# Four chained layers with six state scans on one core: where the state sums of a scan pair are emitted, how other work is rationed, and which engine takes the norms' statistics

## The chip, the cores and the metric

One core of a Trainium2 chip. Times are device microseconds of one execution. Engines: TensorE (PE) multiplies matrices into PSUM, VectorE (DVE), ScalarE (ACT) and GpSimd (POOL) work on elements, SyncE (SP) issues the DMAs. Each engine works through its own queue in order.

## The reference

Everything is float32; x is 2 x 1024 x 256. Four conditioned layers follow each other: a Mamba layer, a layer with one forward and one backward state space model, a linear attention, and a softmax attention with 16 heads of 16. The part that takes most of the time is the state scan, of 512 channels by 16 states by 1024 steps, once in layer 0 and twice in layer 1, for each of two batches (six scans):

```python
def step(h, inp):
    dt_t, B_t, C_t, u_t = inp
    dA = jnp.exp(dt_t[:, :, None] * A)
    h = h * dA + (dt_t * u_t)[:, :, None] * B_t[:, None, :]
    y = jnp.einsum('bdn,bn->bd', h, C_t)
    return (h, y)
...
y = jnp.transpose(ys, (1, 0, 2)) + u * D_param
```

A layer norm stands ahead of every layer, a second one inside layer 1, and one ahead of the output of each attention:

```python
mu = jnp.mean(x, axis=-1, keepdims=True)
var = jnp.mean((x - mu) ** 2, axis=-1, keepdims=True)
return (x - mu) * jax.lax.rsqrt(var + EPS) * g + b
```

## The kernel before

**Tiles of a scan.** A tile holds 32 channels by 4 states on 128 partitions and 1024 steps. A scan has 16 groups of channels times 4 groups of states, 64 tiles; `chain` walks them in pairs: pair p has tiles 2p and 2p+1, two neighbouring channel groups at the same state group k. Eight pairs make one d (128 channels), 32 pairs a scan, and the six scans make 192 pairs. One tile costs:
- `inputs`: e = (dt u) B on GpSimd (L961), into one of eight hb buffers;
- `decay`: dA = exp(dt A) on ScalarE, into one of two PSUM buffers of two banks;
- `tile`: the scan on VectorE (L968 backward, L972 forward), and then the product h C, back into the hb buffer. It runs on VectorE (L975) or, for the first tile of a pair where `far` is set, on GpSimd (L974);
- `fold`: TensorE sums the four states of each channel by a constant matrix, and over the four k in PSUM (L999, two matmuls a tile); at k = 0 `begin` starts the sum with D u (L985, and y of the forward scan in a backward one, L989), reading the buffers fu and fy, of which there is one each. After its sums, an hb buffer is free. `finish` takes the sum out of PSUM three pairs later (L1007, or a copy on ScalarE).

**The order in a pair.** `chain` emits the following by hand, and each engine keeps this order: the next input and the decay of tile 2p+1; a first slot of other work; the sums of pair p-1; the scan and product of tile 2p; the decay of 2p+2, an input and, if far, the product of 2p on GpSimd; a second slot of other work; the scan of tile 2p+1. The variable `lead` keeps VectorE and GpSimd level: it adds 2200 for a pair and what other work spent on VectorE, takes off what other work spent on GpSimd, and at 2300 or more the next pair's product is far (minus 3500). After a far pair the sums are split: those of tile 2p-1 at the usual place, those of 2p-2 behind the second slot. Loads of the next channels (`load_spread`, `load_rest`) stand between these steps on SP's queue.

**Other work.** Norms, projections, convolutions and inputs of the layers to come, and layers 2 and 3 of batch 0, are generators in one queue (`Behind`). Each `yield` ends a step; `slot(columns)` adds columns to a credit and runs steps while the credit is positive and neither ScalarE's nor GpSimd's room is used up. `RATES` has the columns per slot for each of the six scans. A step that yields `ALONE` ends its slot. `until` runs steps at once when something needed is not there yet.

**Norms.** Outside the scans, `stats` takes mean and variance by two instructions per 256-wide row on VectorE. Among the scans, `moments` does it on ScalarE: an Identity with an accumulator for the negated mean and a Square with an accumulator for the variance times 256. `root` (ScalarE) and `refine` (GpSimd among the scans) make the reciprocal root; `scaled` applies it on ScalarE.

After the sixth scan (the tail), layers 2 and 3 of batch 1 and both softmax attentions run; the change leaves their instructions as they are.

Of the kernel before, what the change touches and what calls it, by code (L numbers as in the profile page):

```python
# [18 lines left out]
P = 128  # L19
# [8 lines left out]
SLOT = {"ACT": 2500, "POOL": 1500}  # L28
LEAD = 2300

ALONE = -1

RATES = (2600, 2600, 1250, 1300, 1500, 1500)

LAG = 12

# [20 lines left out]
def kernel(ctx: ExitStack, tc: tile.TileContext, a: dict, out: bass.AP):  # L57
# [339 lines left out]
            nc.vector.bn_aggr(mv[:, j, :], st)  # L397
            spent["DVE"] += 550

    def moments(src, mv):  # L400

        for j in range(0, 4, 2):
            for k in (j, j + 1):
                act_f(
                    small_t((P, 2, D), "t2", 1)[:, 0, :], src[:, k, :], AF.Identity,
                    scale=-1.0 / D, accum_out=mv[:, k, 0:1],
                )
            for k in (j, j + 1):
                act_f(
                    small_t((P, 2, D), "t2", 1)[:, 0, :], src[:, k, :], AF.Square,  # L410
                    bias=mv[:, k, 0:1], accum_out=mv[:, k, 1:2],
                )
            spent["ACT"] += 4 * 250
            yield 320

    def root(mv):

        r = small_t((P, mv.shape[1]), "rstd", 2)
        act_f(r, mv[:, :, 1], AF.Ln, bias=eps, scale=1.0 / D if mode["scans"] else 1.0)
        act_f(r, r, AF.Exp, scale=-0.5)  # L420
        return r

    def refine(mv, r):

        q = small_t((P, mv.shape[1]), "newt", 2)
        e = nc.gpsimd if mode["scans"] else nc.vector
        if mode["scans"]:
            e.tensor_scalar(q, mv[:, :, 1], 1.0 / D, EPS, ALU.mult, ALU.add)
            e.tensor_tensor(q, q, r, ALU.mult)
            e.tensor_tensor(q, q, r, ALU.mult)  # L430
            e.tensor_scalar(q, q, -0.5, 1.5, ALU.mult, ALU.add)
            e.tensor_tensor(r, r, q, ALU.mult)
            e.tensor_tensor(q, mv[:, :, 0], r, ALU.mult)
            spent["POOL"] += 900
            return q
        e.scalar_tensor_tensor(q, mv[:, :, 1], EPS, r, ALU.add, ALU.mult)
        e.scalar_tensor_tensor(q, q, -0.5, r, ALU.mult, ALU.mult)
        e.scalar_tensor_tensor(r, q, 1.5, r, ALU.add, ALU.mult)
        e.scalar_tensor_tensor(q, mv[:, :, 0], -1.0, r, ALU.mult, ALU.mult)
        return q  # L440
# [14 lines left out]
    def normed(src, res):  # L455

        mv = small_t((P, 4 * len(src), 2), "mv", 4)
        for i, t in enumerate(src):
            if mode["scans"]:
                yield from moments(t, mv[:, ts(i, 4), :])  # L460
            else:
                stats(t, mv[:, ts(i, 4), :])
                yield
        r = root(mv)
        yield mode["least"] * 3 // 2
        q = refine(mv, r)
        yield
        for i, t in enumerate(src):
            res.append(scaled(t, r[:, ts(i, 4)], q[:, ts(i, 4)]))
            yield  # L470
# [42 lines left out]
    def projected(w, src, func, bias, res, keep=True, to=None, count=None):  # L513


        def take(m, ch, ps):
            if ch == 0:
                res.append(abuf())
            kw = {} if bias is None else {"bias": bias(m)}
            act_f(res[-1][:, ts(ch, 512)], ps, AF.Identity, **kw)  # L520

        def leave(m):
            if func is AF.Silu:
                silu(res[-1])
            if to is not None:
                save(2, to[ts(m, P), :], res[-1])
            if not keep:
                res.pop()
            if count is not None:
                later(2, lambda: count.append(m))  # L530

        def ended(m, ch, ps):
            take(m, ch, ps)
            held[0] -= 1
            if ch == 1:
                if func is AF.Silu:
                    yield ALONE
                leave(m)
                yield

        waiting = []
        for m in range(4):
            for ch in range(2):
                if len(waiting) == banks["bank"]:
                    yield from ended(*waiting.pop(0))
                waiting.append((m, ch, project(w, src, m, ch)))
                held[0] += 1
                yield
        for v in waiting:
            yield from ended(*v)  # L550
# [110 lines left out]
    def layer0(b, st):  # L661
# [43 lines left out]
        for m in range(4 if b else 0):  # L705

            dgs = abuf((P, 4, P))
            dg = [diag(col("conv_w", 4 * m + j), out=dgs[:, j, :]) for j in range(4)]
            xin, t = abuf(), abuf()

            def conv(ch):
                ps = bank()
                for j in range(4):
                    lag = j if ch == 0 else 0
                    mm(
                        ps[:, lag:], dg[3 - j], xin[:, 512 * ch + lag - j : 512 * ch + 512 - j],
                        start=(j == 0), stop=(j == 3),
                    )
                return ps

            def shifted(ch, ps):
                act_f(t[:, ts(ch, 512)], ps, AF.Identity, bias=col("conv_b", m))

            yield from pipe(
                (lambda: project(w_in[:1], xn, m, 0), lambda ps: act_copy(xin[:, :512], ps)),
                (lambda: project(w_in[:1], xn, m, 1), lambda ps: act_copy(xin[:, 512:], ps)),
                (lambda: conv(0), lambda ps: shifted(0, ps)),
                (lambda: conv(1), lambda ps: shifted(1, ps)),
            )
            yield ALONE  # L730
            silu(t)
            save(2, st["u"][ts(m, P), :], t)
            u.append(t)
            yield
# [6 lines left out]
    def layer1(b, st1, st2):  # L741
# [16 lines left out]
        def first():  # L758
# [5 lines left out]
            for v in skip:  # L764
                nc.vector.tensor_tensor(v, v, twice(cond["s1"][b], 4), ALU.mult)
                far_op(v, v, twice(cond["o1"][b], 4), ALU.add)
                yield ALONE
            yield ALONE
            o = []
            yield from normed(skip, o)  # L770
            for i, v in enumerate(skip):
# [53 lines left out]
    class Behind:  # L825
# [3 lines left out]
        def __init__(self):  # L829
            self.queue = []  # L830
            self.soon = []
            self.credit = 0
            self.alone = False

            self.room = {"ACT": 3400, "POOL": 2300}
            self.given = {"ACT": 0, "POOL": 0}
# [8 lines left out]
        def step(self):  # L845

            while self.queue or self.soon:
                if self.soon and self.soon[0][0] <= 0 and (held[0] == 0 or not self.queue):
                    self.queue.insert(0, self.soon.pop(0)[1])
                if not self.queue:  # L850
                    return 0
                at = work[0]
                try:
                    least = next(self.queue[0])
                    self.alone = least is ALONE
                    return max(work[0] - at, (least if least and least > 0 else mode["least"]))
                except StopIteration:
                    self.queue.pop(0)
            return 0

        def slot(self, columns):
# [3 lines left out]
            if mode["tail"]:  # L865
                for _ in range(columns):
                    self.step()
                return
            self.credit = min(self.credit + columns, 3 * T)
            for key, most in (("ACT", 3400), ("POOL", 2300)):  # L870
                self.room[key] = min(self.room[key] + SLOT[key], most)
            spent.update(ACT=0, POOL=0)
            while (self.queue or self.soon) and self.credit > 0:
# [6 lines left out]
                for key in self.room:  # L880
                    self.room[key] -= spent[key]
                    self.given[key] += spent[key]
                    spent[key] = 0
                if self.alone:
                    break

        def until(self, done):
            while not done():
# [12 lines left out]
    class Scan:  # L901
# [91 lines left out]
        def fold(self, d, cp, k, es):  # L993


            for ch in range(2):
                for j, e in es.items():
                    at = 64 * ch + DS * j
                    nc.tensor.matmul(  # L999
                        self.ys[d, cp][at : at + DS, :], fold, e[:, ts(ch, 512)],  # L1000
                        start=False, stop=(k == NK - 1),
                    )
# [13 lines left out]
    def chain(scans, rates, early, mid, after):  # L1016
# [11 lines left out]
                i, d, cp, k = pairs[n // 2]  # L1028
                made[kind][n] = getattr(scans[i], kind)(4 * d + 2 * cp + n % 2, k)

        def fold(p, js=(0, 1)):
            i, d, cp, k = pairs[p]
            if k == 0 and js[-1]:
                scans[i].begin(d, cp)
            scans[i].fold(d, cp, k, {j: made["inputs"].pop(2 * p + j) for j in js})

        def following(p):

# [18 lines left out]
        ahead(2, "inputs")  # L1057
        mode["scans"] = True
        spent.update(ACT=0, POOL=0, DVE=0)
        lead, far = 0, False  # L1060
        for p, (i, d, cp, k) in enumerate(pairs):
            s = scans[i]
            nxt = following(p)
# [13 lines left out]
            ahead(2 * p + 3, "inputs")  # L1077
            ahead(2 * p + 1, "decay")
            behind.slot(rates[i])

            split = far
            if p:
                fold(p - 1, (1,) if split else (0, 1))

            ended = pairs[p - 3][:3] if p > 2 and k == 2 else None
            if ended and not scans[ended[0]].gate:
# [24 lines left out]
            if k == 1 and nxt:  # L1111
                nxt[0].load_spread(nxt[1] + 1, 1)
            behind.slot(rates[i])
            if split:
                fold(p - 1, (0,))
            s.tile(4 * d + 2 * cp + 1, k, made["decay"].pop(2 * p + 1), made["inputs"][2 * p + 1])
            if final and i + 1 < len(scans):
                scans[i + 1].load_bc(k)
        fold(len(pairs) - 1)
        scans[-1].finish(3, 1)  # L1120
        flush()
# [626 lines left out]
```

## Time and profile before

| | us |
|---|---|
| runs | 2123.51, 2142.31, 2128.95; median 2128.95 |
| profiled execution | 2133.04, its span 2131.3 |
| first scan starts, last scan ends | 70.6, 1488.4 |

Busy time over the span of 2131.3 us:

```profile
PE 1695.2 (80%) x8112; PEld 619.4 (29%) x8112; DVE 1727.9 (81%) x1610; ACT 1207.7 (57%) x1839; POOL 1340.7 (63%) x649
```

Each engine has its busy time, the share of the span and the number of instructions. "PEld" is TensorE's loading of weights, beside its matmuls. [...]

In rows of groups: line, engine, operation, tile written <- tiles read, shapes, count | busy us, mean ns of one | idle us of the engine just before, and who ended it. In rows of waits: engine, tile and line that waited <- engine, tile and line that released it: us in total, times, longest.

### The profile page before, as it was taken

To read this page: it belongs to the slowest core of one execution; us is meant where nothing else is said; L and a number is where in the kernel's file an instruction comes from. 1 tells how busy PE (TensorE), PEld (TensorE's weight loads), DVE (VectorE), ACT (ScalarE), POOL (GpSimd) and SP (SyncE) were. 2 spreads that over 40 slices of the span, in tenths; PEclk is the share of its full clock that TensorE was granted. 3 is DMA by queue.
4 is the path that set the end of the run, shared out by engine and by line. 5 is a ranking of instruction groups with operands and counts; after the bars stand their busy time and mean duration, and the time that the engine had idled before them with its cause. 6 is when DMAs were issued, how large, how long until landed. Compare 5 with 4: busy or idle time off the path is not lost. (4 is left out here: it accounts for less than half of the span.)

```text
span 2131.3 us, 22942 instructions
## 1 busy us (share of the span) xinstructions
PE 1695.2 (80%) x8112; PEld 619.4 (29%) x8112; DVE 1727.9 (81%) x1610; ACT 1207.7 (57%) x1839; POOL 1340.7 (63%) x649
## 2 busy tenths in 40 slices
PE   6476876579888456887885676876999899999997
PEld 3132212123232111222231232310544333333333
DVE  4687798898899889999888898899767756777763
ACT  5557576657646456746456537643044555656665
POOL 0788798898899989999899778998100211000000
PEclk9687977679798556997875767886899999999998
DMA  3654348335583435556744244442300111010001
GB/s 111 233 193 143 105 174 296 115 122 194 202 287 133 168 112 186 174 190 211 286 142 152 98 167 156 138 137 80 119 1 1 38 19 18 24 55 1 1 1 38
DMA packets 106873, 267.55 MB, mean 126 GB/s; under 512 B 14619, under 2 KB 39068, under 8 KB 106757
## 3 DMA queue, kind: packets, MB, share of 16 engines
q1 hardware_dynamic: 106756, 266.07, 36.7%
q8 instruction: 64, 1.05, 0.2%
q14 instruction: 53, 0.43, 0.1%
HBM read 195.90 MB, written 67.90 MB: 124 GB/s over the span
## 5 line engine op out<-in xcount | busy, mean ns | idle before, releaser
L961 POOL TENSOR_TENSOR hb_t<-sp,bc 128x1024 f32<-128x1024 f32 x384 | 920.6, 2440 | 75.9 <-PE ys_t L999 37.5
L135 ACT ACTIVATE dA_t<-sp,negA 128x1024 f32<-128x1024 f32 x384 | 427.8, 1116 | 472.5 <-DVE hb_t L975 379.2
L972 DVE TENSOR_TENSOR_SCAN dA_t<-dA_t,hb_t 128x1024 f32<-128x1024 f32 x202 | 462.0, 2287 | 85.0 <-ACT dA_t L135 60.2
L999 PE MATMUL ys_t<-hb_t,fold 128*32 128x512 f32 x1536 | 378.9, 791 | 183.2 <-DVE hb_t L975 153.4
L1455 DVE TENSOR_REDUCE mh<-sc_t 128x1 f32<-128x512 f32 x512 | 327.5, 684 | 111.5 <-PE sc_t L1446 111.0
L135 ACT ACTIVATE hb_t<-sc_t 128x512 f32<-128x512 f32 x512 | 276.8, 595 | 189.9 <-PE sc_t L1446 189.7
L975 DVE TENSOR_TENSOR hb_t<-dA_t,bc 128x1024 f32<-128x1024 f32 x295 | 361.3, 1225 | 21.8
L1446 PE MATMUL sc_t<-act_t 32*128 32x512 f32 x2048 | 337.6, 653 | 11.2 <-DVE mh L1455 7.3
L974 POOL TENSOR_TENSOR hb_t<-hb_t,bc 128x1024 f32<-128x1024 f32 x89 | 211.6, 2378 | 42.2 <-DVE hb_t L972 30.4
L805 POOL TENSOR_TENSOR act_t<-act_t,row 128x1024 f32<-128x1024 f32 x8 | 18.8, 2349 | 339.4 <-PE sc_t L101 193.3
L968 DVE TENSOR_TENSOR_SCAN dA_t<-dA_t,hb_t 128x1024 f32<-128x1024 f32 x93 | 212.5, 2285 | 11.6 <-ACT dA_t L135 10.5
L999 PEld LDWEIGHTS ys_t<-hb_t,fold 128*32 128x32 f32 x1536 | 49.4, 122 | 451.0 <-DVE hb_t L975 288.7
L1486 PE MATMUL av_t<-hb_t,act_t 128*32 128x256 f32 x2048 | 164.6, 394 | 1.1 <-DVE act_t L1494 1.1
L135 ACT ACTIVATE act_t<-bank_t,cols 128x512 f32<-128x512 f32 (+1 forms) x206 | 130.1, 676 | 56.4 <-PE bank_t L97 54.6
L1446 PEld LDWEIGHTS sc_t<-act_t 32*128 32x128 f32 x2048 | 111.6, 186 | 120.8 <-issue 80.1
L97 PE MATMUL bank_t<-act_t,w_c_w 128*128 128x512 f32 x256 | 125.8, 639 | 22.0 <-ACT act_t L135 21.9
L972 DVE TENSOR_TENSOR_SCAN hb_t<-dA_t,hb_t 128x1024 f32<-128x1024 f32 x54 | 123.1, 2280 | 14.9 <-ACT dA_t L135 14.8
L143 POOL TENSOR_TENSOR act_t<-act_t 128x1024 f32<-128x1024 f32 x50 | 119.5, 2391 | 5.3 <-ACT act_t L135 5.1
L97 PE MATMUL bank_t<-act_t,w_dt_w 64*128 64x512 f32 x96 | 71.8, 878 | 38.5 <-ACT act_t L135 34.7
L1486 PEld LDWEIGHTS av_t<-hb_t,act_t 128*32 128x32 f32 x2048 | 42.2, 108 | 191.4 <-issue 178.7
L101 PE MATMUL bank_t<-ident,act_t 128*128 128x128 f32 x128 | 35.9, 435 | 70.5 <-ACT act_t L135 70.3
L1391 POOL MEMSET act_t<- 128x1024 f32 x8 | 7.6, 951 | 129.5 <-PE sc_t L1446 129.5
(179 smaller groups left out, 1851.4 us busy)
## 6 DMA issues: line engine op xcount, KB each, us to landing
sp<-dt SPq DMA_DIRECT2D x192, 512.0 KB, 5.3
dt<-act_t SPq DMA_DIRECT2D x48, 512.0 KB, 6.2
bc<-bc SPq DMA_DIRECT2D x48, 512.0 KB, 7.5
u<-act_t SPq DMA_DIRECT2D x24, 512.0 KB, 7.4
fu<-u SPq DMA_DIRECT2D x24, 512.0 KB
y<-y SPq DMA_DIRECT2D x96, 128.0 KB, 4.9
g<-act_t SPq DMA_DIRECT2D x16, 512.0 KB, 5.1
fg<-g SPq DMA_DIRECT2D x64, 128.0 KB, 3.9
```

Of the source, the lines that this page charges most:

```text
L97: nc.tensor.matmul(o, w, x, **kw)
L135: nc.scalar.activation(o, x, func, **kw)
L143: nc.gpsimd.tensor_tensor(o, x, y, op)
L961: nc.gpsimd.tensor_tensor(e, self.sp[c, 1], self.bc[0][k], ALU.mult)
L968: nc.vector.tensor_tensor_scan(h[:, ::-1], dA[:, ::-1], e[:, ::-1], 0.0, ALU.mult, ALU.add)
L972: nc.vector.tensor_tensor_scan(h, dA, e, 0.0, ALU.mult, ALU.add)
L974: return lambda: nc.gpsimd.tensor_tensor(e, h, self.bc[1][k], ALU.mult)
L975: nc.vector.tensor_tensor(e, h, self.bc[1][k], ALU.mult)
L999: nc.tensor.matmul(self.ys[d, cp][at : at + DS, :], fold, e[:, ts(ch, 512)], start=False, stop=(k == NK - 1),)
L1446: nc.tensor.matmul(ps, w[r, ts(at, P)], x[r, ts(wide_at, 512)], start=True, stop=True)
L1455: nc.vector.tensor_reduce(mh[n][:, t, ch, j : j + 1], ps, AX.X, ALU.max)
L1486: nc.tensor.matmul(sums.av[32 * j : 32 * j + 32, ts(part, 256)], sts[b]["v"][t // 2][:, t % 2, 4 * g + j, :], es[j // 2][:, at : at + 256] ...
```

## The change

Five parts:
- `fold` of pair p-1 moves from the middle of pair p to its end, behind the second slot and behind the second tile; the split after a far pair goes.
- `RATES` of the first two scans go from 2600 to 2048, and the credit's cap from 3 x 1024 to 2 x 1024 columns.
- `ALONE` goes: these steps become plain yields, which no longer end a slot.
- `moments` goes: among the scans too, the norms take `stats` on VectorE, all four rows of a tile of 4 x 256 in one step.
- `root` and `refine` follow the new form of the statistics; `refine` among the scans has one more GpSimd instruction.

```diff
-RATES = (2600, 2600, 1250, 1300, 1500, 1500)
+RATES = (2048, 2048, 1250, 1300, 1500, 1500)
...
-    def moments(src, mv):
...
-        act_f(r, mv[:, :, 1], AF.Ln, bias=eps, scale=1.0 / D if mode["scans"] else 1.0)
+        act_f(r, mv[:, :, 1], AF.Ln, bias=eps)
...
         if mode["scans"]:
-            e.tensor_scalar(q, mv[:, :, 1], 1.0 / D, EPS, ALU.mult, ALU.add)
+            e.tensor_scalar(q, mv[:, :, 1], EPS, None, ALU.add)
...
-            e.tensor_tensor(q, mv[:, :, 0], r, ALU.mult)
+            e.tensor_scalar(q, mv[:, :, 0], -1.0, None, ALU.mult)
+            e.tensor_tensor(q, q, r, ALU.mult)
...
         for i, t in enumerate(src):
-            if mode["scans"]:
-                yield from moments(t, mv[:, ts(i, 4), :])
-            else:
-                stats(t, mv[:, ts(i, 4), :])
-                yield
+            stats(t, mv[:, ts(i, 4), :])
+            yield
...
                 if func is AF.Silu:
-                    yield ALONE
+                    yield
...
-            yield ALONE
+            yield
             silu(t)
...
                 far_op(v, v, twice(cond["o1"][b], 4), ALU.add)
-                yield ALONE
-            yield ALONE
+                yield
...
-                    self.alone = least is ALONE
-                    return max(work[0] - at, (least if least and least > 0 else mode["least"]))
+                    return max(work[0] - at, least or mode["least"])
...
-            self.credit = min(self.credit + columns, 3 * T)
+            self.credit = min(self.credit + columns, 2 * T)
...
-                if self.alone:
-                    break
...
             behind.slot(rates[i])
-            split = far
-            if p:
-                fold(p - 1, (1,) if split else (0, 1))
...
             behind.slot(rates[i])
-            if split:
-                fold(p - 1, (0,))
             s.tile(4 * d + 2 * cp + 1, k, made["decay"].pop(2 * p + 1), made["inputs"][2 * p + 1])
             if final and i + 1 < len(scans):
                 scans[i + 1].load_bc(k)
+            if p:
+                fold(p - 1)
         fold(len(pairs) - 1)
```

## The prediction

> **What bounds the kernel now.** I read first the table of busy times by stretch, cut where the last scan ends on VectorE (1488 us), because the change touches only the scans' stage and the attention behind it keeps its instructions.
>
> ```profile
> core 0: us, PE busy (x) PEld busy (x) DVE busy (x) ACT busy (x) POOL busy (x), PEclk, DMA share, GB/s
> 70.00:1488.00 1418.00, 1043.15 (x3292) 349.28 (x3292) 1263.92 (x762) 837.57 (x1183) 1279.65 (x601) 0.77 0.49 170
> 1488.00:2131.00 643.00, 609.89 (x4712) 248.40 (x4712) 438.76 (x806) 335.14 (x605) 54.23 (x34) 0.96 0.10 26
> ```
>
> In the 1418 us of scans VectorE (DVE) is busy 89% and GpSimd (POOL) 90%: two engines share the bound, and the code keeps them level by hand ("far" products). ScalarE (ACT, 59%) and TensorE (PE, 74%) have room. From 1488 us on TensorE is 95% busy and nothing there changes, so I carry 643 us over and argue about the 1418 alone.
>
> Second, who VectorE and GpSimd wait for in that stage (line, releaser, us in total, times, longest):
>
> ```profile
> DVE dA_t L972 <- ACT dA_t L135: 60.2, 27, 5.9
> DVE dA_t L972 <- POOL hb_t L961: 24.8, 11, 13.3
> DVE hb_t L972 <- ACT dA_t L135: 14.8, 5, 5.8
> DVE act_t L812 <- PE bank_t L97: 12.1, 5, 4.7
> ```
>
> ```profile
> POOL hb_t L961 <- PE ys_t L999: 37.5, 18, 8.6
> ```
>
> With two smaller rows (10.5 and 3.0) VectorE waits 88.5 us for ScalarE's exponentials, 25.8 for GpSimd, 19 for TensorE. GpSimd waits 37.5 us because the state sums (L999) have not yet freed one of the eight hb buffers. Third, the groups by shape, for prices (busy us, mean ns):
>
> ```profile
> L961 POOL TENSOR_TENSOR hb_t<-sp,bc 128x1024 f32<-128x1024 f32 x384 | 920.6, 2440 | 75.9 <-PE ys_t L999 37.5 <-DMA bc<-bc 19.1 <-DVE y L1007 7.7
> ...
> L975 DVE TENSOR_TENSOR hb_t<-dA_t,bc 128x1024 f32<-128x1024 f32 x295 | 361.3, 1225 | 21.8
> ...
> L974 POOL TENSOR_TENSOR hb_t<-hb_t,bc 128x1024 f32<-128x1024 f32 x89 | 211.6, 2378 | 42.2 <-DVE hb_t L972 30.4 <-DVE hb_t L968 11.7
> ...
> L135 ACT ACTIVATE t<-act_t,mv 128x256 f32<-128x256 f32 x64 | 32.5, 508 | 2.1
> ...
> L135 ACT ACTIVATE t<-act_t 128x256 f32<-128x256 f32 x64 | 26.2, 409 | 1.1
> ...
> L396 DVE BATCH_NORM_STATS2 st<-act_t 128x6 f32<-128x256 f32 x48 | 19.2, 400 | 1.9 <-DMA act_t<-in_x 1.9
> ...
> L397 DVE BATCH_NORM_AGGREGATE mv<-st 128x2 f32<-128x6 f32 x48 | 8.7, 182 | 1.6
> ```
>
> **Norms' statistics.** Counting instructions in the two built programs: 64 rows' worth of statistics leave ScalarE and reach VectorE, 48 statistics become 112. VectorE gains 64 x (0.400 + 0.182) = 37.2 us. ScalarE loses 64 x (0.508 + 0.409 + 2 x 0.187 for the two accumulator reads) = 82.6 us. Of VectorE's waits for ScalarE, only two (scans 182 and 183, 1.6 and 0.9 us) lie behind such statistics; the others lie behind evictions, silu tables and the eight scalings of a norm, which stay. So ScalarE's relief is worth 2.5 us, not 82.6. The code answers the 37.2 us by its balance: `lead` counts the statistics and sends more products to GpSimd. The built programs have 89 far products before and 99 after. VectorE: 37.2 - 10 x 1.225 = **+25.0 us**. GpSimd: 10 x 2.378 + 8 small operations x 0.2 = **+25.4 us**. Both bounds rise alike.
>
> How much of the 25 shows depends on how unevenly it falls. I priced every engine's instructions between two scans by the rows above (a scan 2.285), added up groups of consecutive pairs, and took the larger of VectorE and GpSimd in each group. Example, pairs 38 to 41 (layer 1's two norms of batch 0): before 30.0 (6.5 + 5.8 + 10.7 + 7.0 on VectorE) against 29.9 on GpSimd; after 38.3 (12.5 + 7.7 + 12.3 + 5.8) against 38.0. Over the stage: all in one sum 1302 before and 1328 after (+25); groups of four pairs 1377 and 1412 (+35); single pairs 1470 and 1518 (+48). The measured 1418 lies between the last two kinds, eight hb buffers being about three pairs of lookahead, so I take groups of four: **+35**, ends +25 and +48.
>
> A rule speaks against moving more products to GpSimd. VectorE's 295 products last 1223 to 1226 ns, with GpSimd busy 90% of the stage, so I charge no contention. The Trainium skill ("GPSIMD Engine Reference", Specifications) has the two engines share SBUF interfaces, with contention when a VectorE instruction has two SBUF inputs; by it ten more GpSimd products could hold VectorE ten times, and the sum would be some 24 us higher.
>
> **State sums at the end of the next pair.** Before, the sums of pair p-1 stand on TensorE between the two slots of other work of pair p (or half of them at the end, where a product was far); after, all four, with `begin`'s two to four matmuls, stand behind both slots. Nothing is added. What it can give: TensorE's other matmuls no longer queue behind a sum that waits for VectorE (153.4 us of TensorE's waiting, 65 times). But when ScalarE waited for an eviction's bank, TensorE was mostly running that slot's own matmuls; sums running inside those waits come to about 20 us, half of the waits reach VectorE: at most -10. What it can cost: hb buffers come free later. Setting, in the trace, each sum behind the last other matmul of its second slot, the input that reuses its buffer would be late 54 times by 134 us in all, never over 11.4. These are not additive: a dense stretch loses its lead once, by about 5 us, and the median lead of an input over its scan is 8.3 us. In the stretches where GpSimd has no lead (around 300, 570, 690, 980 us) the buffers have 10 us and more to spare, so there it costs nothing. I take one loss of 5 us at three or four of the stretches, less 8 for the freed matmuls: **+8**, ends -10 and +45 (a third of 134). `begin` frees the fu and fy buffers later too, and the next loads of these, on SP's queue, stand right behind it: 24 times, half a pair (3.7 us) later each, with the spread loads queued after them. Those are needed one and a half pairs (11 us) later and land in 5.3, so this is covered; if not, it costs as the waits for sp do today (ScalarE 34.4 us in 7 waits, of which 6 us reached VectorE): +3 at the high end. The gated finish on VectorE comes three pairs behind and keeps over a pair of cover.
>
> **Rations.** 2600 becomes 2048 columns a slot for the first two scans, the credit is capped at two instead of three rows of 1024, and a slot no longer ends at `ALONE`. 2048 columns (four matmuls of 512, two rows of the trace each) take 3.70 us at best, in the timeline at 525 us, half a pair 3.51 (2.285 + 1.225). Half-pairs with over 2048 columns of other work fall from 20 to 10, and the columns above that from 27,600 to 8,700, most of it in the first two scans, where VectorE waits 62 of its 88.5 us. The 12,800 columns fewer there are 23 us of TensorE; I take half of it for VectorE's waits: **-10**, ends 0 and -41 (two thirds of 62). Against it, the 20 silus of these stages now share their slot with the eviction ahead of them, 0.68 us each, where a table load already makes VectorE wait: **+4**, ends 0 and 14.
>
> A second rule bears on the clock. The stage's granted clock is 0.77, the attention's 0.96; waits for sums average 2.4 us, the longest 6.5, and a wait for GpSimd's product reaches 6.5; I leave the clock as it is. The Trainium skill ("TensorE: Matmul & The Clock Gate", What's actually happening) has the clock halve after an idle window of some 3.4 us; one collected wait a pair would then hold it at half, TensorE's 1043 busy us would become 1043 x 0.77 / 0.5 = 1606, more than the stage lasts, and the sum some 190 us higher.
>
> **Sum.** 35 - 2.5 + 8 - 10 + 4 = +34. The profiled execution took 2133.0 us (span 2131.3, 1.7 around it), 4 above the median 2128.95 of the runs; on the median the forecast is 2163.
>
> **Rivals.**
> - Faster: TensorE's slots were the true cause of VectorE's waits. Place: 70 to 600 us, where ScalarE waits 73 us for TensorE's banks and VectorE 62 for ScalarE. If two thirds go, 25 - 41 = -16: 2113. It decides once more than 35 us of the 88.5 go. For it: 4096-column slots nearly vanish; against: silu tables and norm scalings (some 38 us of the 88.5) stay. Chance 0.10.
> - No change seen: the added VectorE work falls into its 130 us of waiting, as both engines sit idle a tenth of the time: 2129 to 2140. Against it: the two idle at different times, and a wait for ScalarE ends only after VectorE's own product. Chance 0.22.
> - Worse: the late sums starve GpSimd of buffers in the dense stretches, and a third of the 134 us reaches VectorE: 34 - 8 + 45 = +71, 2200. For it: GpSimd waits 18 times for sums already. Chance 0.13.
> - That the change does not do what it says is excluded by the built program: the counts above are its own.
>
> My forecast, both engines 25 us fuller and less even, has 0.55; its own range is 2143 to 2183. The range 2118 to 2200 takes in the ends of the terms and leaves out the far half of the fast rival and of the slow one, some 2 in 10 with the tails. About 1% (21 us, the spread of the three runs being 19) can be told from no change: below 2108 0.07, within 0.28, above 2150 0.65.
>
> **What would show it.** In the changed profile, up to the last scan: VectorE some 25 us busier, GpSimd too, ScalarE 83 less; the stage near 1452 us instead of 1418 and the attention again 643. TensorE's waits for products shrink or gather at the pair's end; GpSimd's wait for ys_t grows from 37.5 to 50 or 80. VectorE's wait for ScalarE below 50 would prove the fast rival's mechanism; GpSimd's wait for ys_t over 100, with VectorE waiting for hb_t over 60, the slow one's. I am wrong in kind if the stage is no longer while VectorE's busy time has grown.

## The result, and the profile after

The changed kernel takes 2119.66 us in the median of 16 runs (2109.82 to 2130.65), the kernel before 2140.16 in 16 (2123.51 to 2144.44). The ratio is 0.9916, with a 95% interval of 0.9899 to 0.9933: 18 us faster, where 34 us slower was forecast. Of the three runs of before that the prediction had seen, two are the fastest of the sixteen, so their median of 2128.95, on which the forecast stands, is 11 us low.

The profiled execution has a span of 2115.4 us, 15.9 under that of before. The two stretches, cut where the last scan now ends (columns as in the prediction):

```profile
70.00:1475.00 1405.00, 976.72 (x3292) 348.63 (x3292) 1281.65 (x881) 769.58 (x927) 1295.73 (x618) 0.77 0.50 171
1475.00:2115.00 640.00, 608.00 (x4712) 247.46 (x4712) 438.12 (x805) 335.40 (x605) 53.76 (x34) 0.96 0.10 26
```

The scans take 1405 us instead of 1418 (forecast: 1452), although VectorE is 18 us busier (1263.92 before) and GpSimd 16 (1279.65). ScalarE is 68 us less busy and TensorE 66, the latter with as many matmuls as before. The attention differs by 3 us, with unchanged instructions.

The waits of VectorE, GpSimd, TensorE and ScalarE that answer to those of before over the whole execution:

```profile
PE ys_t L974 <- POOL hb_t L949: 101.1, 25, 8.4
...
PE ys_t L974 <- DVE hb_t L950: 52.4, 21, 7.1
POOL hb_t L936 <- PE ys_t L974: 52.0, 20, 12.3
...
ACT act_t L133 <- PE bank_t L95: 39.6, 25, 3.9
...
DVE dA_t L947 <- ACT dA_t L133: 35.1, 18, 4.7
...
DVE dA_t L947 <- POOL hb_t L936: 27.1, 12, 13.7
...
DVE act_t L791 <- PE bank_t L95: 24.5, 7, 7.9
```

VectorE's first row was 60.2 us in 27 waits; with the smaller rows of the same kind its waits for ScalarE fall from 99 to 45 us over the scans' stage (from 88.5 to 44 for exponentials alone). It waits more for GpSimd (25.8 to 40.4 us) and for TensorE (19 to 27). GpSimd's wait for the sums grows from 37.5 to 52.0. TensorE still waits 153 us for products (183 before), now mostly for the far ones, at the end of the pair. ScalarE waits 39.6 us for TensorE's banks; before it was 60.8.

The groups:

```profile
L936 POOL TENSOR_TENSOR hb_t<-sp,bc 128x1024 f32<-128x1024 f32 x384 | 908.8, 2399 | 88.5 <-PE ys_t L974 52.0
...
L950 DVE TENSOR_TENSOR hb_t<-dA_t,bc 128x1024 f32<-128x1024 f32 x285 | 349.1, 1225 | 21.4 <-DVE dA_t L947 0.5
...
L949 POOL TENSOR_TENSOR hb_t<-hb_t,bc 128x1024 f32<-128x1024 f32 x99 | 235.7, 2381 | 19.6 <-DVE hb_t L947 17.8
```

The 285 and 99 products are the counts that the prediction worked with, at the same prices: 1225 ns on VectorE in both kernels, so the ten more far products did not slow VectorE's own.

The six scans take 242, 251, 231, 218, 240 and 225 us; before 260, 250, 231, 217, 247 and 213. The largest gain is in the first one. There, in the built program of before, four slots of the convolutions hold 4,090 columns each. ScalarE and TensorE in that stretch of the kernel before (start us, duration us, instruction and how many rows of it, [idle before <- releaser]):

```profile
219.58 0.69 ACT L135 ACTIVATE act_t<-bank_t,cols 128x512 f32<-128x512 f32 x1 [2.26 <-PE bank_t L97]
225.20 0.69 ACT L135 ACTIVATE act_t<-bank_t,cols 128x512 f32<-128x512 f32 x1 [4.93 <-PE bank_t L97]
225.79 1.11 ACT L135 ACTIVATE dA_t<-sp,negA 128x1024 f32<-128x1024 f32 x1
```

```profile
219.47 1.08 PE L985 MATMUL ys_t<-fu,dgD 64*64 64x512 f32 x4
220.48 1.05 PE L999 MATMUL ys_t<-hb_t,fold 128*32 128x512 f32 x4
221.46 3.70 PE L97 MATMUL bank_t<-act_t 128*128 128x512 f32 x8
225.09 1.91 PE L999 MATMUL ys_t<-hb_t,fold 128*32 128x512 f32 x12
```

Inside ScalarE's wait of 4.93 us (220.27 to 225.20) TensorE runs the last 1.2 us of `begin` and sums, and then the 3.7 us of the convolution whose bank ScalarE evicts. The exponential stands behind that eviction and ends at 226.9; VectorE had waited 3.24 us for it. Pairs 16 to 23, in which these convolutions fall, last 72.7 us before and 58.7 after. The largest loss is in pairs 160 to 167 (58.3 to 73.4 us): residual additions on VectorE stand there behind TensorE's banks, the last row of the waits above.

### The profile page after: what moved, and what is told of

The parts are those of the page before. It is cut to its first block, busy times and chain, and to the rows that moved or that the text cites. A ratio compares the mean times of both kernels' runs of the same rounds, so it can differ in the third digit from the quotient of the medians.

```text
span 2115.4 us, 22775 instructions
## 1 busy us (share of the span) xinstructions
PE 1626.8 (77%) x8112; PEld 617.7 (29%) x8112; DVE 1745.5 (83%) x1728; ACT 1140.4 (54%) x1583; POOL 1356.9 (64%) x667
## 3 DMA queue, kind: packets, MB, share of 16 engines
q8 instruction: 64, 1.05, 0.2%
## 4 chain that ended last, share of the span: by engine, by line
PE 30%; DVE 10%; POOL 5%; issue 4%; ACT 2%; DMA 0%; DVEq 0%; ACTq 0%; POOLq 0%
PE sc_t L1418 13%; PE av_t L1458 6%; PE sc_t L95 4%; POOL hb_t L936 3%; PE bank_t L95 3%; DVE dA_t L943 2%; DVE mh L1427 2%; PE sc_t L99 2%; DVE dA_t L947 2%; POOL hb_t L949 1%; PE ys_t L974 1%; DVE hb_t L943 1%; ACT act_t L133 1%; POOL act_t L141 1%; DVE hb_t L947 1%
## 5 line engine op out<-in xcount | busy, mean ns | idle before, releaser
L936 POOL TENSOR_TENSOR hb_t<-sp,bc 128x1024 f32<-128x1024 f32 x384 | 908.8, 2399 | 88.5 <-PE ys_t L974 52.0
L947 DVE TENSOR_TENSOR_SCAN dA_t<-dA_t,hb_t 128x1024 f32<-128x1024 f32 x195 | 445.9, 2287 | 62.3 <-ACT dA_t L133 35.1
L974 PE MATMUL ys_t<-hb_t,fold 128*32 128x512 f32 x1536 | 294.2, 781 | 153.5 <-POOL hb_t L949 101.1
L950 DVE TENSOR_TENSOR hb_t<-dA_t,bc 128x1024 f32<-128x1024 f32 x285 | 349.1, 1225 | 21.4 <-DVE dA_t L947 0.5
L949 POOL TENSOR_TENSOR hb_t<-hb_t,bc 128x1024 f32<-128x1024 f32 x99 | 235.7, 2381 | 19.6 <-DVE hb_t L947 17.8
L943 DVE TENSOR_TENSOR_SCAN dA_t<-dA_t,hb_t 128x1024 f32<-128x1024 f32 x90 | 205.7, 2285 | 9.2 <-POOL hb_t L936 6.0
L974 PEld LDWEIGHTS ys_t<-hb_t,fold 128*32 128x32 f32 x1536 | 40.5, 123 | 358.9 <-POOL hb_t L949 139.5
L947 DVE TENSOR_TENSOR_SCAN hb_t<-dA_t,hb_t 128x1024 f32<-128x1024 f32 x61 | 139.0, 2279 | 3.9 <-ACT dA_t L133 3.6
L95 PE MATMUL bank_t<-act_t,w_dt_w 64*128 64x512 f32 x96 | 74.6, 912 | 40.4 <-ACT act_t L133 34.4
```

The costliest lines, as they stand in the source:

```text
L95: nc.tensor.matmul(o, w, x, **kw)
L936: nc.gpsimd.tensor_tensor(e, self.sp[c, 1], self.bc[0][k], ALU.mult)
L943: nc.vector.tensor_tensor_scan(h[:, ::-1], dA[:, ::-1], e[:, ::-1], 0.0, ALU.mult, ALU.add)
L947: nc.vector.tensor_tensor_scan(h, dA, e, 0.0, ALU.mult, ALU.add)
L949: return lambda: nc.gpsimd.tensor_tensor(e, h, self.bc[1][k], ALU.mult)
L950: nc.vector.tensor_tensor(e, h, self.bc[1][k], ALU.mult)
```

## The experiments

The five parts were taken alone and in combination. F is the late sums, r the rates of 2048, c the cap of two rows (R is r and c), A the missing `ALONE`, N the statistics on VectorE with their root. FRAN is the changed kernel; a set of letters is the kernel before with these parts. The ratio is to the kernel before on the same chip, from 6 to 16 runs of a kernel, and a difference of two ratios is known to about 0.0035, or 7 us of 2140. "Scan 0" and "scan 1" are the us of the first two scans, "wait" is VectorE's wait for ScalarE in the scans' stage. These three come from one profiled execution of each kernel, and that one can lie off the median: R's is 11 us below its own, A's 10, FRN's 12 and that of the rate 1792 9 us above.

### Each part alone

F, the late sums:

```diff
-            split = far
-            if p:
-                fold(p - 1, (1,) if split else (0, 1))
...
+            if p:
+                fold(p - 1)
```

> The kernel before with one part of the change: the state sums behind both slots of the next pair, no split. Theory 'rations' (smaller slots took away ScalarE's waits for TensorE in the first two scans): nothing much here, 0 to +8 us, GpSimd's wait for ys_t up from 37 to 50 or more. Theory 'sums' (TensorE's other matmuls no longer stand behind a sum that waits for VectorE): most of the gain is here, -15 to -30 us, VectorE's wait for ScalarE down from 88 to below 60. Theory 'statistics': 0.

R, the rations:

```diff
-RATES = (2600, 2600, 1250, 1300, 1500, 1500)
+RATES = (2048, 2048, 1250, 1300, 1500, 1500)
...
-            self.credit = min(self.credit + columns, 3 * T)
+            self.credit = min(self.credit + columns, 2 * T)
```

> The kernel before with one part: 2048 columns a slot in the first two scans and the credit capped at two rows. Theory 'rations': -15 to -30 us, the first scan 15 us shorter, ScalarE's waits for TensorE's banks shorter. Theory 'sums': 0 to -5. Theory 'statistics': 0 to -5.

A, the steps that end a slot:

```diff
-                    yield ALONE
+                    yield
```

> The kernel before with one part: ALONE steps are plain yields, a slot no longer ends there. All three theories: within 5 us of the kernel before; by the prediction's term +4 (0 to +14), as a silu shares its slot with the eviction ahead of it.

N, the statistics:

```diff
-            if mode["scans"]:
-                yield from moments(t, mv[:, ts(i, 4), :])
-            else:
-                stats(t, mv[:, ts(i, 4), :])
-                yield
+            stats(t, mv[:, ts(i, 4), :])
+            yield
```

> The kernel before with one part: the norms' statistics among the scans on VectorE. By the prediction's term +25 to +48 us, VectorE busy 25 us more in the scans' stage. Theory 'rations' and theory 'sums': +10 to +35. Theory 'statistics' (ScalarE's relief of 83 us is what ended VectorE's waits): -10 to -25.

| part | median us | ratio, 95% | scan 0 | scan 1 | wait |
|---|---|---|---|---|---|
| F | 2141.47 | 1.0008 (0.9990 to 1.0025) | 255 | 246 | 93 |
| R | 2150.84 | 1.0053 (1.0034 to 1.0073) | 240 | 265 | 95 |
| A | 2129.52 | 0.9959 (0.9939 to 0.9979) | 258 | 253 | 99 |
| N | 2149.06 | 1.0038 (1.0022 to 1.0054) | 261 | 257 | 75 |

In us these are +2, +11, -9 and +8: together +12, while the whole change brings -18. The parts do not add up. F came out as the expectation's first theory has it (GpSimd's wait for sums is 69 us); for R and A no theory came true, and N lies just under its range of +10 to +35. R shows a cost that was not counted: it shortens scan 0 by 20 us and loses 15 in scan 1. There VectorE and ScalarE do this:

```profile
518.01 1.23 DVE L975 TENSOR_TENSOR hb_t<-dA_t,bc 128x1024 f32<-128x1024 f32 x1
548.66 2.30 DVE L972 TENSOR_TENSOR_SCAN dA_t<-dA_t,hb_t 128x1024 f32<-128x1024 f32 x1 [29.43 <-ACT dA_t L135]
```

```profile
525.91 0.69 ACT L135 ACTIVATE act_t<-bank_t,cols 128x512 f32<-128x512 f32 x1 [2.75 <-PE bank_t L97]
529.35 0.69 ACT L135 ACTIVATE act_t<-bank_t,cols 128x512 f32<-128x512 f32 x1 [2.75 <-PE bank_t L97]
532.78 0.69 ACT L135 ACTIVATE act_t<-bank_t,cols 128x512 f32<-128x512 f32 x1 [2.75 <-PE bank_t L97]
...
547.43 1.13 ACT L135 ACTIVATE dA_t<-sp,negA 128x1024 f32<-128x1024 f32 x1
```

VectorE stands still for 29.4 us, and ScalarE takes one eviction after another, each after 2.75 us of waiting for the next bank, until the exponential comes. In the built program 13,312 columns stand there, at the head of pair 60: with smaller rations the projections are not done when the next scan's loads need them, and `until` runs the rest at once. Over the whole stage half-pairs with more than 2048 columns are 20 before, 11 in R and 10 in FRAN, which has no such lump.

### All parts but one

> The changed kernel with the rations as before (2600, cap of three rows), sums late, no ALONE, statistics on VectorE. Theory 'rations, but only where the other work keeps up': the gain is gone, 0 to +12 us against the kernel before, five slots of 4096 and more columns in the first scan, VectorE waiting 60 us or more for ScalarE. Theory 'sums': still -15 to -20. Theory 'ALONE' (what its removal alone gave, -9, is all there is): -5 to -12.

> The changed kernel with the sums as before, in the middle of the pair and split after a far one. Theory 'rations': -12 to -25 us against the kernel before, like the changed kernel. Theory 'sums late pay only behind small slots': the gain falls to -5 or less.

> The changed kernel with the statistics on ScalarE again. Theory 'rations': -20 to -40 us against the kernel before, better than the changed kernel by the 17 us of VectorE work that it does without; if ScalarE's relief is a part of the gain after all (theory 'statistics'), 0 to -8.

> The changed kernel with the ALONE steps that end a slot. No lump of over 3072 columns at the end of the second scan, unlike the rations alone (13312 columns). Theory 'rations': -8 to -20 us against the kernel before; if ALONE's removal is what makes small slots pay, 0 or slower.

| kernel | median us | ratio, 95% | scan 0 | scan 1 | wait |
|---|---|---|---|---|---|
| FAN, no rations | 2139.60 | 1.0002 (0.9984 to 1.0019) | 261 | 248 | 76 |
| RAN, sums as before | 2126.73 | 0.9934 (0.9908 to 0.9960) | 241 | 259 | 50 |
| FRA, no statistics | 2120.75 | 0.9913 (0.9887 to 0.9939) | 248 | 244 | 78 |
| FRN, `ALONE` kept | 2131.55 | 0.9968 (0.9944 to 0.9992) | 246 | 250 | 72 |
| FRAN | 2119.66 | 0.9916 (0.9899 to 0.9933) | 242 | 251 | 45 |

Against FRAN the rations are worth -18 us, the missing `ALONE` -11, the late sums -4 (within the noise), and the statistics, forecast at +32, cost +1. The theory 'rations' had FAN and RAN right, but FRA was to gain 20 to 40 us by it and gains 19, no more than FRAN; FRN, with -7, lies just short of its -8 to -20. What the statistics do is to be seen in the stage of FRA (its last scan ends at 1478 us, so the first row has 7 us of the attention in it; then VectorE's waits):

```profile
70.00:1485.00 1415.00, 991.02 (x3315) 345.05 (x3315) 1265.07 (x764) 834.37 (x1183) 1283.30 (x603) 0.76 0.50 170
```

```profile
DVE dA_t L971 <- ACT dA_t L135: 40.7, 18, 7.7
...
DVE hb_t L971 <- ACT dA_t L135: 15.6, 9, 6.9
```

Cut at each kernel's own last scan, VectorE is busy 1262 us in FRA and 1282 in FRAN, 20 more; its waits for ScalarE are 78 and 45, 33 less (with the smaller rows). So the load came, and waits of more than its size went with it.

### The load by itself, and the rations taken apart

In the first of these, FRAN takes each statistic among the scans twice on VectorE, the first time into scratch, and ScalarE's work stays:

```diff
         for i, t in enumerate(src):
+            if mode["scans"]:
+                stats(t, small_t((P, 8), "newt", 2).rearrange("p (a b) -> p a b", b=2))
             stats(t, mv[:, ts(i, 4), :])
```

> The changed kernel with every statistic among the scans taken twice on VectorE (the first time into a scratch tile), the other work's order and slots the same. VectorE gets 37.2 us more, 6 more far products take 7.3 off and give GpSimd 14. By the prediction's term (VectorE and GpSimd bind alike, no slack): +22 to +45 us against the changed kernel, +4 to +27 against the kernel before. If VectorE has slack there, as the measured zero of the statistics suggests: 0 to +10 against the changed kernel, -18 to -8 against the kernel before.

RA, rA and cA have A with both rations, with the rates alone and with the cap alone.

> The kernel before with two parts: rations and no ALONE; sums and statistics as before. Theory 'smaller slots that keep up' (the gain needs both: slots of over 4000 columns gone, and no lump of work forced at the end of a scan): -12 to -20 us against the kernel before, nearly all of the change's gain. If the late sums are a third part of it: -4 to -10.

> As s1, but of the rations only the rates of the first two scans (2048); the cap stays at three rows. Half-pairs above 2048 columns are 16 with 20,968 columns in excess (before 20 and 27,624; s1 10 and 9,710). Theory: half the way, -8 to -14 us; if the lower rates are the cause, like s1.

> As s1, but of the rations only the cap of two rows; the rates stay at 2600. Half-pairs above 2048 columns are 12 with 9,704 in excess, as few as in s1. Theory: like s1, -12 to -20 us, since what counts is how much a slot can take at once; if the lower rates are the cause, like the removal of ALONE alone, -9.

| kernel | median us | ratio, 95% | scan 0 | scan 1 | wait |
|---|---|---|---|---|---|
| FRAN, statistics twice | 2137.95 | 0.9995 (0.9976 to 1.0013) | 243 | 258 | 45 |
| RA | 2136.20 | 1.0000 (0.9980 to 1.0020) | 243 | 250 | 79 |
| rA | 2134.49 | 0.9976 (0.9961 to 0.9991) | 251 | 258 | 104 |
| cA | 2125.79 | 0.9937 (0.9917 to 0.9957) | 249 | 250 | 86 |

The second set of statistics costs 17 us (0.9995 less 0.9916). In its profile, groups:

```profile
L952 DVE TENSOR_TENSOR hb_t<-dA_t,bc 128x1024 f32<-128x1024 f32 x279 | 341.7, 1225 | 20.7 <-DVE dA_t L945 0.5
...
L394 DVE BATCH_NORM_STATS2 st<-act_t 128x6 f32<-128x256 f32 x128 | 50.8, 397 | 3.8 <-POOL act_t L141 3.8
...
L395 DVE BATCH_NORM_AGGREGATE newt<-st 128x2 f32<-128x6 f32 x64 | 11.7, 182 | 2.2
```

`lead` answers again with more far products (279 products stay on VectorE instead of 285), VectorE is 27 us busier (1282 to 1309) and GpSimd 25 (1296 to 1320). So 27 us of load, with the wait for ScalarE unchanged at 45, costs 17, less than the 22 to 45 that the prediction's term gave and more than the 10 of the other reading: VectorE and GpSimd bound the stage, but not wholly.

The cap, with A, is the cheapest good version: -13 of the 18 us with one ration and the missing `ALONE`, and its interval overlaps that of FRAN. RA, which has as few large slots as FRAN and was to bring nearly all of its gain, brings none, and rA brings 5 where 8 to 14 were expected.

### Rates and statistics together

Four more kernels take the rates back to 2600, with and without the cap, the late sums and the statistics. FcAN is the changed kernel but for this line:

```diff
-RATES = (2048, 2048, 1250, 1300, 1500, 1500)
+RATES = (2600, 2600, 1250, 1300, 1500, 1500)
```

> Sums late, cap of two rows and no ALONE; the rates stay at 2600 and the statistics on ScalarE. Theory 'the cap is the ration that counts, the lower rates only slow the catching up': -20 to -32 us against the kernel before, at least as good as the changed kernel (-18). If the late sums add nothing by themselves: like s3, -13. If the lower rates are needed with late sums: 0 to -10.

> As x1 with the statistics on VectorE, that is the changed kernel with its rates back at 2600. Theory 'cap': -15 to -28 us. By half of the price that doubling the statistics gave (17 us for 27 us more of VectorE work), x1 is better than x2 by 3 to 12 us.

> Sums late and no ALONE, the rations as before: half-pairs of up to 5114 columns in the first scan. Theory 'late sums pay only behind small slots': no better than the removal of ALONE alone, -9 to 0 us. If the late sums pay once no slot ends early: -15 to -25.

> As x2 with the sums as before, in the middle of the pair. With x1, s3 and x2 it gives the late sums' effect behind small slots twice: theory 'late sums pay behind small slots': 5 to 15 us worse than x2. If they add nothing: like x2, within 4 us.

| kernel | median us | ratio, 95% | scan 0 | scan 1 | wait |
|---|---|---|---|---|---|
| FcA | 2129.15 | 0.9962 (0.9940 to 0.9985) | 253 | 250 | 89 |
| FcAN | 2159.75 | 1.0101 (1.0068 to 1.0134) | 263 | 256 | 85 |
| FA | 2134.62 | 0.9974 (0.9954 to 0.9995) | 262 | 250 | 102 |
| cAN | 2154.08 | 1.0064 (1.0038 to 1.0090) | 262 | 252 | 89 |

The theory that the cap is the ration that counts fails here: it gave FcA -20 to -32 us (measured -8) and FcAN -15 to -28. FcAN, with one constant changed, is 40 us slower than FRAN and 22 slower than the kernel before; cAN was to be as slow or slower and is 8 us faster, near the noise. FcAN's waits of VectorE:

```profile
DVE dA_t L953 <- ACT dA_t L135: 66.1, 25, 8.8
DVE dA_t L953 <- POOL hb_t L942: 29.6, 15, 12.4
```

These are nearly the rows of the kernel before, with VectorE's load on top. So there are six pairs of kernels that differ by the statistics alone. The last column is the second less the third: what the load would have cost if each us of waiting saved were a us of time.

| pair | time, us | change of the wait, us | difference |
|---|---|---|---|
| none to N | +8 | 99 to 75: -24 | 32 |
| FA to FAN | +6 | 102 to 76: -27 | 33 |
| RA to RAN | -14 | 79 to 50: -29 | 15 |
| FRA to FRAN | +1 | 78 to 45: -33 | 34 |
| cA to cAN | +27 | 86 to 89: +3 | 24 |
| FcA to FcAN | +30 | 89 to 85: -5 | 35 |

Where the waits for ScalarE fall, the statistics cost little or gain; where they do not, they cost about what was forecast. The waits are those of single executions, so this is a pattern of six pairs and not yet a cause.

### The rate of the first scan

FRAN with the first rate alone lowered further:

```diff
-RATES = (2048, 2048, 1250, 1300, 1500, 1500)
+RATES = (1792, 2048, 1250, 1300, 1500, 1500)
```

and, in the second, 1536.

> The changed kernel with 1792 columns a slot in the first scan instead of 2048. The built program has 6 half-pairs above 2048 columns instead of 10 (3,584 columns in excess instead of 8,680), and no lump at the end of the scan. Theory 'the rate of the first scan decides how long it takes, as long as the other work keeps up': the first scan 235 to 242 us (before 260, changed kernel 242), -20 to -28 us against the kernel before. If the gain of 2048 was a chance of where the steps fall: anywhere from -18 to +10, and the first scan above 246.

> The changed kernel with 1536 columns a slot in the first scan: the other work falls behind, and 6,144 columns are forced in one half-pair, in pair 27. Theory: the lump gives back 8 to 15 us, by the row of the rations alone (a lump of 13,312 columns made VectorE wait 29.4 us); the first scan 245 to 255 us, -14 to 0 us against the kernel before. If lower rates are better in any case: below y1.

They take 2134.79 us (0.9969, 0.9946 to 0.9993) and 2145.70 (1.0027, 1.0008 to 1.0046), with scan 0 at 250 and 256 us and waits of 62 and 66. Half-pairs over 2048 columns are 6 and 8, fewer than FRAN's 10, and yet both are slower: counting large slots does not order the times. The second has a lump of 6,144 columns at the head of pair 28, and VectorE waits 19 us there in one piece; the first has none of that kind, and what slows it was not found. Of the two readings set down for it, the one that fits is the second, that the gain of 2048 was a chance of where the steps fall (-18 to +10 us, first scan above 246).

## Why the prediction was wrong

**The step that failed** is the relief in "Norms' statistics": "So ScalarE's relief is worth 2.5 us, not 82.6." I looked for statistics right ahead of an exponential that VectorE waited for, found two, and took all other waits for fixed, as they lay behind evictions, tables and scalings "which stay". The instructions stayed and their waits did not: in four of the six pairs of kernels VectorE's waits for ScalarE fell by 24 to 33 us, and there the statistics, forecast at +32 with the relief, measured between -14 and +8. (ScalarE's busy time fell by 68 us, not the 83 forecast.)

Why the waits fell is not shown. One reading is the order of ScalarE's queue: work taken from it lets evictions, silus and exponentials behind it come earlier. But from cA to cAN and from FcA to FcAN ScalarE's busy time falls as much (837 to 771 and 836 to 770 us), and the waits do not. The rival is the cut of the slots: `stats` is one step of 640 columns where `moments` is two of 320, and it uses none of ScalarE's room, so the work behind it moves to earlier slots. From FRA to FRAN 12 of the 33 us fall in pairs 16 to 23 (17.4 to 5.1 us), where neither kernel takes a statistic and where the built programs cut the convolutions otherwise: the first scan has two slots of 4,090 columns and one of 3,066 in FRA, one and three in FRAN. No run moves the statistics and keeps the slots.

**The load** was priced right as busy time: +25 was forecast for each engine, N alone has +26 and +25, the changed kernel +18 and +16. Its cost of +35 (25 to 48) stands against 17 us for 27 us in the direct test, and 15 to 35 by the table of pairs. So the "groups of four pairs" overrate it in the direct test; by this alone the sum would still have been above zero.

**Rations**, -10 (0 to -41): the first scan shortened with smaller slots as the prediction has it (260 to 240 us in R). The size depends on the rest. Rates and cap together are worth -18 us (FAN to FRAN), -13 (FA to FRA), +9 (A to RA) and +11 alone. The rates in the company of cap, A and N are worth -40 us with the late sums (FcAN to FRAN) and -28 without them (cAN to RAN); without N they are worth -10 (FcA to FRA) and +13 (cA to RA). So the term holds in two of four companies, and in the others it lies above its high end: I gave no place to other work that falls behind and comes back as one lump. That `until` forces what is late stands in the code, and the prediction did not count it.

**`ALONE`**, +4 (0 to 14): wrong in sign. In four comparisons its removal gained 7 to 11 us (alone, F to FA, R to RA, FRN to FRAN). I charged silus sharing a slot with an eviction. The other side, which I left out, is that an ended slot keeps its credit and the next one is larger: half-pairs over 2048 columns fall from 20 to 18, and with the cap to 12, by the built programs. Whether that is the cause stays open, as the wait for ScalarE is 99 us with and without A.

**Late sums**, +8 (-10 to +45): six pairs of kernels with and without them give +2, +3, +5, +8, -4 and -19 us, mostly within the noise. GpSimd's wait for sums grew as forecast (37.5 to 52.0, forecast 50 to 80), and the slow rival's signs, over 100 and over 60, did not appear. The -19 (RA to FRA) was not explained. "Nothing is added" was true of the instructions; that TensorE would be 66 us less busy I did not see (below).

**The rival that came nearest** is the fast one, given 0.10: "VectorE's wait for ScalarE below 50 would prove the fast rival's mechanism", and it is 45 us. That sign proves less than I said. The rival asked for two thirds of 62 us in the first two scans, and about half went (64 to 32 with the smaller rows). And it named TensorE's slots as the cause: without N the wait stays at 78 or more, with N and the old rates at 75 or more; rates and N together, and A, have 45 to 50. And "wrong in kind if the stage is no longer while VectorE's busy time has grown" is what happened. That 2119.66 lies inside the range of 2118 to 2200 is luck: the range was laid around a slower kernel and from a median that was 11 us low.

**Two readings beside the sum** were off as well. The products of VectorE do not have two SBUF inputs, as the sentence on contention takes for granted: h lies in one of the PSUM buffers. And the late sums do not bring "one collected wait a pair": TensorE waits for products 46 times in 192 pairs, 77 times before (the last section).

**What stays open.** Why rates and statistics need each other, and why 1792 is worse than 2048, the runs do not show. Only the pairs of kernels are measured; with steps that come to lie elsewhere in every kernel, part of these 18 us may be where the steps happen to fall.

## What to carry to other kernels

When work leaves an in-order queue, ask what becomes earlier behind it and what its leaving does to the cut of other work, not only which waits stand directly behind it: here 68 us off an engine that is 59% busy went with 24 to 33 us fewer waits of an engine that bounds the stage in four pairs of kernels, and with none in two. A change of slot sizes is to be judged with the largest forced lump in view: 2048 columns a slot gained 20 us in one scan and lost 15 to a single wait in the next. And parts that steer one schedule are to be measured in the company they ship in: alone these four came to +12 us, together to -18, and one constant was worth 40.

## What the runs showed of the hardware

The sums of both tiles of a pair, issued in turn, take no longer than the sums of one tile. TensorE's sums in the kernel before, after far pairs (a matmul leaves two rows in the trace, as 768 sums are 1536 rows; x4 is two matmuls of one tile), and in the changed kernel (x8 is four of two tiles):

```profile
640.78 1.05 PE L999 MATMUL ys_t<-hb_t,fold 128*32 128x512 f32 x4 [0.73 <-POOL hb_t L974]
...
652.60 1.05 PE L999 MATMUL ys_t<-hb_t,fold 128*32 128x512 f32 x4 [0.47 <-POOL hb_t L974]
```

```profile
198.83 1.06 PE L974 MATMUL ys_t<-hb_t,fold 128*32 128x512 f32 x8
199.82 3.70 PE L95 MATMUL bank_t<-act_t 128*128 128x512 f32 x8
203.46 1.06 PE L974 MATMUL ys_t<-hb_t,fold 128*32 128x512 f32 x8
```

1.05 us for two and 1.06 for four, and the next matmul starts 0.99 us after the four (0.98 after the two at 220.48 us above). The two tiles write different 32 of the 128 rows, and their matmuls run beside each other. The Trainium skill ("TensorE: Matmul & The Clock Gate", Part 3, packing small matmuls) describes such overlap of tiles of the array. All sums, before and after:

```profile
L999 PE MATMUL ys_t<-hb_t,fold 128*32 128x512 f32 x1536 | 378.9, 791 | 183.2 <-DVE hb_t L975 153.4
```

```profile
L974 PE MATMUL ys_t<-hb_t,fold 128*32 128x512 f32 x1536 | 294.2, 781 | 153.5 <-POOL hb_t L949 101.1
```

The nine kernels with split sums have 379 to 394 us of them, the eleven with late ones 288 to 316. TensorE was not the bound: F alone has 995 us of TensorE in the stage instead of 1043, and its time is 1.0008.

The late sums do lower the granted clock a little. Averaged over a kernel's runs, the clock of the whole execution falls in each of the six pairs of kernels with and without them, by 0.005 (RA to FRA) to 0.021 (cAN to FcAN); F alone has 0.822 against 0.829. In the stage of the change's own two profiles it is 0.77 both times. There the clock takes two values only, full and half, and half holds for 643 of 1418 us before and for 641 of 1405 after. The rule that the prediction weighed (the same page, What's actually happening: half clock after an idle window of about 3.4 us) is not tested by the change: TensorE's idle times of over 3.4 us in the stage are 38 before and 42 after, far from one a pair.

VectorE's products last 1224 or 1225 ns on average in each of the twenty profiles, with 89 to 105 products on GpSimd. The contention rule of "GPSIMD Engine Reference" (Specifications) names VectorE instructions with two SBUF inputs, and these products have one, the other being in PSUM; so no run here tests it.
